# Graph attention, two layers: denominators of the last block summed by ones, its last output bank finished in two parts

## The chip, the cores and the metric

The kernel runs on one core of one Trainium2 chip, in one launch. The metric is the device time of an execution in microseconds (us); the median of several runs is compared. The engines are named as in the profile: PE is TensorE's matmul, PEld its loading of weights, DVE is VectorE, ACT is ScalarE, POOL is GpSimd, SP is SyncE (here only a queue for transfers).

## The reference

The input is a node matrix `x` of 4096 x 512 and an adjacency matrix of 4096 x 4096 of zeros and ones. Layer 0 is an encoder and decoder with sigmoid attention. Layer 1, in which the change lies, is graph attention with four heads of 128 features:

```python
    def _L1_gnn_ref(X, A, W, b, a_self, a_neigh):
        ...
        feats = jnp.einsum('nf,hfo->hno', X, W)
        e_s = jnp.einsum('hno,ho->hn', feats, a_self)
        e_n = jnp.einsum('hno,ho->hn', feats, a_neigh)
        logits = e_s[:, :, None] + e_n[:, None, :]
        logits = jnp.where(logits > 0, logits, LRELU_ALPHA * logits)
        logits = logits + NEG_INF * (1.0 - A)[None, :, :]
        attn = jax.nn.softmax(logits, axis=-1)
        out = jnp.einsum('hnm,hmo->hno', attn, feats)
        out = out + b[:, None, :]
        ...
        return jax.nn.relu(out)

    # --- layer 1 (adj_preln) ---
    h = jnp.maximum(_layernorm(x, axis=-1), 0.0)
    x = x + _L1_gnn_ref(h, adj, L1_gnn_W, L1_gnn_b, L1_gnn_a_self, L1_gnn_a_neigh)
```

For every head and target node the kernel needs two sums over all 4096 neighbours: the weighted sum of features, and the sum of the weights, by which it divides (the denominator).

## The kernel before, in words

All three attentions go through one function, `attention`. A block is one head and one half of the target nodes (TB = 2048 of them), so each attention has eight blocks. Inside a block the loop runs over 32 tiles `j` of 128 neighbours. One step makes a weight tile `e` of 128 neighbours x 2048 targets and uses it:

- SP loads the mask tile `a` (five buffers, so tile j's load waits for the release of tile j - 5).
- ACT computes a ReLU of the scores into `e` (L1045), and DVE adds a column and multiplies by the mask (L1046, the "mask product"). The pool has nine buffers for `e`.
- PE multiplies the feature block of tile `j` with `e` and accumulates into four banks `po` of 128 x 512 (L470). A matmul in float32 appears in the profile as two records.
- For the denominator each tile goes one of three ways, by the entry of the block in a table (`GAT_FIRST`, `GAT`, `GAT_LAST`): "moved" tiles are added into a buffer `w` by POOL's accumulating transfers (L490); tiles "by ones" are summed on PE against a column block of ones (L268, `add_to_den`, four matmuls of 32 columns into one bank `den`); all others are added on DVE into `acc` (L500; the profile calls its memory `R`). At the end of the block `w` and `acc` are summed by ones into `den` too.

Engines run their instructions in the order that a scheduler wrote down; a wait holds up everything behind it on the same engine.

The last block of the last attention ends differently from the others. Its last four tiles, 28 to 31, are not multiplied in the loop. They are kept in `late`, and their products come after the sums by ones, bank by bank (L533), so that PE has work while the denominators go their way: DVE copies `den` adding a small constant (L546) and inverts it (L547), SP stores the four rows to memory as `rinvs` (L549) and loads them back four times, spread over all partitions (L552). These spread rows are written over `acc`, which is free by then. Then `finish_gat` takes each bank in turn: DVE adds `ssum` and multiplies by the spread inverse (L1065), takes the maximum with the negative bias and adds the residual (L1066), and SP stores the result (L1067). The end of the program waits for these stores.

In this block `GAT_LAST` sends the odd tiles 3 to 23 to POOL and tiles 30 and 31 to the sums by ones; the other nineteen are added on DVE. A list `at_end` exists that holds additions back until all 32 mask products have been issued, but only for the encoder, by the condition `kept is not None`:

```python
                        if last and kept is not None and j >= NJ - 6:
                            at_end.append(e)
```

Of the kernel before, what the change touches and what calls it, by code (L numbers as in the profile page):

```python
# [34 lines left out]
ALU = mybir.AluOpType  # L35
# [4 lines left out]
N, F, H, D, P = 4096, 512, 4, 128, 128  # L40
IB = 512
NIB = N // IB
NJ = N // P
C = IB // P

TB = 2048
NTB = N // TB
SB = TB // IB
# [18 lines left out]
GAT_FIRST = (0, 2, 4, 6, 8, 10, 12, 14, 16, 18, 20, 22, 24), (30, 31)  # L67
GAT = tuple(range(3, 28, 2)), (31,), True

GAT_LAST = (3, 5, 7, 9, 11, 13, 15, 17, 19, 21, 23), (30, 31)  # L70

KEEP = 5

# [17 lines left out]
def kernel(ctx, tc, x, xT, adjT, w0, w0T, v0, wencT, wdecT, vecs, w1, w1T, a1, outT):  # L91
    nc = tc.nc
# [8 lines left out]
    R = [RS[:, i, :] for i in range(5)]  # L101
# [3 lines left out]
    def nodes(r, ib):  # L105
        return r[:, ib * IB:(ib + 1) * IB]

    def block(r, j):
        return r[:, j * D:(j + 1) * D]

    def bank():
        return psum.tile([P, IB], FP, name="ps")
# [111 lines left out]
    def attention(what, keep, pools, weights, values, row_of, out, finish, ebufs, modes=None, invert=None,  # L224
                  kept=None, sums=None, sums2=None, extras={}, row0=None, masks0=(), in_parts0=1,
                  finish_last=None, behind=(), fast=None):
# [38 lines left out]
        def add_to_den(den, t, start=False, stop=False):  # L265
            nonlocal last_ones
            for s in range(SB):
                last_ones = nc.tensor.matmul(den[s * 32:(s + 1) * 32, :], ones[:, 0:32], t[:, s * IB:(s + 1) * IB],  # L268
                                             start=start, stop=stop)
# [20 lines left out]
        def spread(h, tb, s):  # L290

            rb = spool.tile([P, IB], FP, name="rb", bufs=3 if fast is None else 2)
            hop.dma_start(rb, everywhere(rinvs[h][tb], 0, s * IB, IB))  # L293
            return rb

        def at(j, f, *args):

            later.setdefault(j, []).append(lambda: f(*args))
# [97 lines left out]
        for n, (h, tb) in enumerate(blocks):  # L396
            last = n == len(blocks) - 1
# [5 lines left out]
            if fast is None:  # L403
                po = [bank() for _ in range(SB - 1)]
            else:
                po, aux = (banks8[(n + k) % 2 * SB:((n + k) % 2 + 1) * SB] for k in range(2))
                if tb == 0:
                    fast[2](h)
            ahead, late = [], []
            adds, held, stores, at_end, next_row = [], [], [], [], None  # L410
            for j in range(NJ):
# [13 lines left out]
                else:  # L425
# [11 lines left out]
                    if stores and (store if n > 1 else j % KEEP == KEEP - 3):  # L437
                        k, t = stores.pop()
# [47 lines left out]
                if invert is not None:  # L486
                    if j in moved:

                        for into_half, e_half in in_parts(2, into, e):
                            nc.gpsimd.dma_start(into_half, e_half, **({"accum_op": ALU.add} if j > moved[0] else {}))  # L490
                    elif j in by_ones:
                        held.append(e)
                    else:
                        adds.append(e)
                        if last and kept is not None and j >= NJ - 6:
                            at_end.append(e)
                        elif len(adds) == 2:
                            nc.vector.tensor_add(acc, *adds)
                        elif len(adds) > 2:
                            nc.vector.tensor_add(acc, acc, e)  # L500

                    if j == NJ - 1:
                        for t in at_end:
                            nc.vector.tensor_add(acc, acc, t)

                    if held and j + 1 not in by_ones:
                        with tc.issue_after(last_main.ins):
                            for t in held:
                                add_to_den(den, t, not begun)
                                begun = True  # L510
                        held = []
                    if j == NJ - 1:
                        with tc.issue_after(last_ones.ins) if last_ones is not None else nullcontext():
                            if moved and not ends_later:
                                add_to_den(den, into, not begun)
                                begun = True
                            add_to_den(den, acc, not begun, not ends_later)
# [5 lines left out]
            if not last:  # L523

                at(EVICT if fast is None else 3, ending, h, tb, po, den if invert is not None else None,
                   4 if kept == "write" and n == 0 else 0)
                if ends_later:
                    at(1, add_to_den, den, into, False, True)
                rowb = next_row
                continue  # L530
            for s, b in enumerate(po):
                for k, t in late:
                    nc.tensor.matmul(b, block(values[h], k), t[:, s * IB:(s + 1) * IB], start=(k == 0),  # L533
                                     stop=(k == NJ - 1))
            if fast is not None:
                combined(h, tb, m)
            outs = [out(spool, h, tb, s, po[s]) for s in range(SB)] if finish_last is None else po
            if invert is None:
                for s, o in enumerate(outs):
                    rb = spread(h, tb, s)  # L540
# [11 lines left out]
                queue.dma_start(rb, everywhere(rinvs[h][tb], 0, s * IB, IB))  # L552
            for s, rb in enumerate(rbs):
                if finish_last is not None:
                    finish_last(h, tb, s, po[s], rb)
                    continue
                for f in finish:
                    f(spool, h, tb, s, outs[s], rb, True)

    def in_parts(n, *tiles):  # L560
        for i in range(n):
            yield tuple(t[:, i * TB // n:(i + 1) * TB // n] for t in tiles)
# [10 lines left out]
    with tc.tile_pool(name="keep", bufs=1) as keep:  # L573

        with tc.tile_pool(name="f_small", bufs=1) as small, tc.tile_pool(name="f_work", bufs=2) as work:
# [5 lines left out]
            for ib in range(NIB):  # L581
# [7 lines left out]
                for c in range(0, C, 1 if ib == 0 else C):  # L589
                    n = 1 if ib == 0 else C  # L590
# [11 lines left out]
            for ib in range(NIB):  # L602
# [34 lines left out]
                if ib == 0:  # L637

                    pw = bank1()
                    with tc.issue_after(last_pe.ins):  # L640
                        for h in range(H):
                            nc.tensor.matmul(pw[:, 2 * h:2 * h + 2], w0Ts[:, h, :], v0s[:, h, :],
                                             start=True, stop=True)
# [4 lines left out]
                for c in range(C):  # L648
                    j = ib * C + c
                    for k in range(2):  # L650
                        pv = heads_of(bank())
                        for h in range(2):
                            nc.tensor.matmul(pv[:, h, :], hT[:, 2 * k + h, c * P:(c + 1) * P], w0x[:, 2 * k + h, :],
                                             start=True, stop=True)
# [75 lines left out]
        with tc.tile_pool(name="enc", bufs=1) as spool:  # L730

            with tc.issue_after(last_copy.ins), tc.issue_after(masks0[-1][1].ins):
                attention("enc", keep, spool, tanh_weights, R[0:4], lambda h, tb: (rows[tb], h), out_enc,
                          (scaled, statistics), 6, lambda n: (ENC_FIRST, ENC_SECOND, ENC_THIRD, ENC)[min(n, 3)],
                          (TINY, ALU.max), "write", row0=row0, masks0=masks0,
                          extras={(2, 8): encoder_weights, (H * NTB - 1, 1): coefs_of_three,
                                  (H * NTB - 1, 4): bias_of_three, (H * NTB - 1, 6): scale_three,
                                  (H * NTB - 1, 9): product_ahead(0), (H * NTB - 1, 12): product_ahead(1)})
# [100 lines left out]
        with tc.tile_pool(name="dec", bufs=1) as spool:  # L839
            attention("dec", keep, spool, tanh_weights, xc, lambda h, tb: (rows[tb], h), out_dec, (scaled, elu), 5,  # L840
                      kept="read", behind=behind_it, fast=(z, xd, stationaries),
                      extras={(H * NTB - 1, 28): decoder_weights})
# [8 lines left out]
    with tc.tile_pool(name="l_small", bufs=1) as small, tc.tile_pool(name="l_work", bufs=2) as work:  # L851
# [41 lines left out]
        for fb in range(C):  # L893
            with tc.issue_after(last_pe.ins):
                for h in range(H):
                    k = 2 * (fb * H + h)
                    last_pe = nc.tensor.matmul(pw[:, k:k + 2], w1Ts[:, h, fb * P:(fb + 1) * P], a1s[:, h, :],
                                               start=True, stop=True)
# [62 lines left out]
        for ib in range(NIB):  # L961
            for c in range(C):
# [9 lines left out]
                j = ib * C + c  # L972
# [85 lines left out]
        nc.scalar.activation(o, o, AF.Relu, bias=vec_of("b")[:, h:h + 1])  # L1058
        nc.gpsimd.dma_start(nodes(outT[h * P:(h + 1) * P, :], tb * SB + s), o, accum_op=ALU.add)

    def finish_gat(h, tb, s, po, rb):

        x1b, nb = x1_last
        o = R[2][:, TB + s * IB:TB + (s + 1) * IB]
        nc.vector.scalar_tensor_tensor(o, po, ssum[:, h:h + 1], rb, ALU.add, ALU.mult)  # L1065
        nc.vector.scalar_tensor_tensor(o, o, nb, x1b[:, s * IB:(s + 1) * IB], ALU.max, ALU.add)  # L1066
        nc.sync.dma_start(nodes(outT[h * P:(h + 1) * P, :], tb * SB + s), o)  # L1067

    with tc.tile_pool(name="gat", bufs=1) as spool:
        x1_last = []  # L1070

        def load_last(load):
            x1_last.append(spool.tile([P, TB], FP, name="rowb", bufs=2))
            nc.sync.dma_start(x1_last[0], outT[(H - 1) * P:H * P, (NTB - 1) * TB:NTB * TB])
            x1_last.append(edge.tile([P, 1], FP, name="nb"))
            nc.vector.tensor_scalar_mul(x1_last[1], vec_of("b")[:, H - 1:H], -1.0)

        def add_bias(load):
            nc.scalar.activation(x1_last[0], x1_last[0], AF.Identity, bias=vec_of("b")[:, H - 1:H])

        with tc.issue_after(last_pe.ins):
            attention("gat", spool, spool, gat_weights, v1, lambda h, tb: (rowsg, tb * H + h), out_gat,
                      (scaled_gat, add_to_output), 7, lambda n: (GAT_FIRST, *[GAT] * (H * NTB - 2), GAT_LAST)[n],
                      (N * TINY, ALU.add), sums=R[2][:, 0:TB], sums2=(row0, R[2][:, TB:N]), row0=row0, in_parts0=3,
                      extras={(0, 1): rest_of_rows, (H * NTB - 1, NJ - 10): load_last, (H * NTB - 1, NJ - 4): add_bias},
                      finish_last=finish_gat)
# [42 lines left out]
```

## Time and profile before

| what | value |
|---|---|
| time, median of 3 runs | 3191.79 us (3190.47 to 3193.64) |
| the profiled execution's own time | 3192.33 us |
| its span | 3190.4 us, 30044 instructions |
| PE busy | 3139.7 us, 98% of the span, 10531 records |
| DVE busy | 2938.4 us, 92%, 2222 instructions |
| ACT busy | 2573.5 us, 81% |
| POOL busy | 522.3 us, 16% |
| mean PE clock over the span | 0.998 of full speed |

The profile is of one execution. Its times count from the start of its span, which is some 2 us shorter than the time of that execution; the end of the span is at 3190.4. A line such as L1046 is a line of the kernel before. Names are the program's (`e`, `den`, `acc`), and where a tile is a view of a larger memory, the larger one's name is shown: `R` holds `acc`, the spread inverses and the outputs of the last block. Busy shares are averages over a program with many stages. The last block runs from about 3065 us on (its first products on PE), and what matters for the change lies in its last 50 us, where the timeline of each engine and the chain of waits are read.

### The profile page before, as it was taken

How to read it: one execution, taken by the hardware profiler on the slowest of the kernel's cores; microseconds unless marked ns; L12 is line 12 of the kernel's file. 1: busy time of each engine (PE TensorE's matmuls, PEld its weight loads, DVE VectorE, ACT ScalarE, POOL GpSimd, SP SyncE). 2: the span in 40 equal slices, each digit the busy share in tenths (PEclk: the TensorE clock that was granted, in tenths of full speed). 3: DMA queues.
4: the chain of work that ended last, by engine and by line, in shares of the span. 5: the costliest groups of instructions: out<-in, count | busy, mean ns of one | idle time of the engine just before them, and what ended most of it. 6: DMA issues, size and time to landing. Idle time of an engine off the chain costs nothing.

```text
span 3190.4 us, 30044 instructions
## 1 busy us (share of the span) xinstructions
PE 3139.7 (98%) x10531; PEld 1368.4 (43%) x10531; DVE 2938.4 (92%) x2222; ACT 2573.5 (81%) x1825; POOL 522.3 (16%) x679
## 2 busy tenths in 40 slices
PE   7999999999999999999999999999999999999998
PEld 6334444444444463333333333458544444444443
DVE  7989999999998778999999999785699999999998
ACT  7999999999998449999999999466755665666663
POOL 3001211211211000010100100026312222222211
PEclk9999999999999999999999999999999999999999
DMA  9999978988987014444544454322579999899996
GB/s 211 199 194 254 267 209 232 268 223 231 264 226 200 20 47 146 160 164 148 166 162 161 139 169 145 104 98 74 151 191 229 216 222 242 220 211 232 233 210 163
DMA packets 215343, 590.28 MB, mean 185 GB/s; under 512 B 25912, under 2 KB 29016, under 8 KB 199192
## 3 DMA queue, kind: packets, MB, share of 16 engines
q0 software_dynamic: 70976, 231.94, 38.0%
q1 hardware_dynamic: 132200, 332.53, 30.3%
q10 hardware_dynamic: 12016, 23.90, 2.1%
q8 instruction: 82, 1.34, 0.2%
q14 instruction: 69, 0.57, 0.1%
HBM read 379.20 MB, written 84.30 MB: 145 GB/s over the span
## 4 chain that ended last, share of the span: by engine, by line
PE 54%; DVE 21%; issue 12%; ACT 8%; DMA 4%; DVEq 0%; POOL 0%; ACTq 0%; POOLq 0%; SPq 0%
PE ps L332 22%; PE ps L470 14%; PE ps L718 7%; DVE e L1046 6%; DVE R L500 6%; ACT e L566 5%; DVE e L568 4%; PE den L332 3%; PE ps L951 3%; DVE acc L500 3%; ACT e L567 3%; DMA a<-mask 3%; PE den L268 1%; PE ps L800 1%; DMA acc<-e 1%
## 5 line engine op out<-in xcount | busy, mean ns | idle before, releaser
L470 PE MATMUL ps<-e,R 128*128 128x512 f32 x3992 | 1736.8, 595 | 21.3 <-DVE e L568 17.2
L470 PEld LDWEIGHTS ps<-e,R 128*128 128x128 f32 x3992 | 754.0, 190 | 1000.1 <-issue 923.4
L568 DVE TENSOR_TENSOR e<-e,a 128x2048 f32<-128x2048 f32 (+1 forms) x470 | 1049.5, 2260 | 78.6 <-ACT e L567 65.1
L566 ACT ACTIVATE e<-rowb,score 128x2048 f32<-128x2048 f32 (+1 forms) x470 | 909.2, 1969 | 20.6 <-PE ps L332 9.0
L567 ACT ACTIVATE e<-e 128x2048 f32<-128x2048 f32 (+1 forms) x470 | 866.6, 1879 | 6.5 <-DVE e L568 3.2
L332 PE MATMUL ps<-e,R 128*64 128x512 f32 x2624 | 746.8, 592 | 1.6 <-DVE e L568 1.5
L1045 ACT ACTIVATE e<-rowb,nq,jcol 128x2048 f32<-128x2048 f32 x224 | 459.8, 2088 | 263.5 <-DMA w<-e 130.8
L1046 DVE SCALAR_TENSOR_TENSOR e<-e,jcol,a 128x2048 f32<-128x2048 f32 (+1 forms) x265 | 591.8, 2264 | 2.8 <-ACT e L1045 2.8
L332 PEld LDWEIGHTS ps<-e,R 128*64 128x64 f32 x2624 | 241.9, 137 | 319.8 <-issue 316.2
L500 DVE TENSOR_TENSOR R<-R,e 128x2048 f32<-128x2048 f32 x128 | 291.6, 2278 | 0.0
L500 DVE TENSOR_TENSOR acc<-acc,e 128x2048 f32<-128x2048 f32 x122 | 278.6, 2283 | 1.0
L490 POOL DMA_DIRECT2D w<-e x178 | 149.1, 847 | 611.9 <-DMA w<-e 335.1
L718 PE MATMUL ps<-R,w 128*128 128x512 f32 x512 | 220.8, 592 | 0.6 <-DVE w L692 0.6
L490 POOL DMA_DIRECT2D acc<-e x142 | 119.1, 893 | 518.5 <-DMA acc<-e 232.2
L718 PEld LDWEIGHTS ps<-R,w 128*128 128x128 f32 x512 | 97.1, 190 | 123.0 <-issue 116.7
L332 PE MATMUL den<-e,R 128*64 128x512 f32 x320 | 149.8, 592 | 0.0
L332 PE MATMUL ps<-e,w 128*64 128x512 f32 x288 | 138.1, 592 | 0.7 <-DVE e L568 0.7
L293 POOL DMA_DIRECT2D rb<-rinvs x60 | 34.5, 579 | 518.8 <-DVE R L682 453.6
L951 PE MATMUL ps<-w1x,hT 128*128 128x260 f32 x512 | 115.5, 384 | 1.4 <-ACT hT L929 1.4
L332 PE MATMUL ps<-t,w 128*64 128x512 f32 x336 | 111.2, 592 | 1.1 <-DVE t L341 1.1
L951 PEld LDWEIGHTS ps<-w1x,hT 128*128 128x128 f32 x512 | 96.5, 190 | 19.9 <-issue 3.4
L332 PE MATMUL ps<-t,R 128*64 128x512 f32 x192 | 90.2, 592 | 0.0
(205 smaller groups left out, 2103.9 us busy)
## 6 DMA issues: line engine op xcount, KB each, us to landing
a<-mask SPq DMA_DIRECT2D x720, 256.0 KB, 4.3
w<-e POOLq DMA_DIRECT2D x178, 512.0 KB, 6.7
acc<-e POOLq DMA_DIRECT2D x142, 512.0 KB, 7.0
e<-ekeep SPq DMA_DIRECT2D x48, 1024.0 KB, 5.0
ekeep<-e SPq DMA_DIRECT2D x36, 1024.0 KB, 8.3
mask<-in_adjT POOLq DMA_DIRECT2D x8, 2048.0 KB, 106.0
rowb<-rows SPq DMA_DIRECT2D x16, 1024.0 KB, 7.5
rb<-rinvs POOLq DMA_DIRECT2D x60, 256.0 KB, 4.6
```

The costliest lines, as they stand in the source:

```text
L293: hop.dma_start(rb, everywhere(rinvs[h][tb], 0, s * IB, IB))
L332: last_half = nc.tensor.matmul(b[g * HD:(g + 1) * HD, :], weight, x, start=start, stop=stop)
L470: last_main = nc.tensor.matmul(b, block(values[h], j), e[:, s * IB:(s + 1) * IB], start=(j == 0), stop=(j == NJ - 1))
L490: nc.gpsimd.dma_start(into_half, e_half, **({"accum_op": ALU.add} if j > moved[0] else {}))
L500: nc.vector.tensor_add(acc, acc, e)
L566: nc.scalar.activation(e, rowb, AF.Tanh, bias=column(score[:, 1], j, h), scale=0.5)
L567: last_act = nc.scalar.activation(e, e, AF.Exp, scale=0.5)
L568: last_dve = nc.vector.tensor_mul(e, e, a)
L718: last = nc.tensor.matmul(z, w[:, fb, o * P:(o + 1) * P], nodes(src[fb], ib), start=(fb == 0), stop=(fb == C - 1))
L951: m = nc.tensor.matmul(banks[k][:, 0:2 * DX], hT[:, fb, c * P:(c + 1) * P], w1x[:, fb, 2 * k:2 * k + 2, :].rearrange("p h x -> p (h x)"), ...
L1045: last_act = nc.scalar.activation(e, rowb, AF.Relu, bias=column(nq, j, h), scale=column(jcol, j, h))
L1046: last_dve = nc.vector.scalar_tensor_tensor(e, e, column(jcol2, j, h), a, ALU.add, ALU.mult)
```

## The change

Three things are altered, all in the last block of the last attention.

Tiles 28 and 29 are summed by ones on PE as tiles 30 and 31 are, and no longer added on DVE. The additions of tiles 26 and 27 stay on DVE, but come after the mask products of all tiles, since the condition on `at_end` no longer asks for the encoder. (For the encoder nothing changes; the decoder has no denominators.) And the last of the four banks is handled in two halves of 256 columns: its late products, its two finishing instructions, and its store.

```diff
-GAT_LAST = (3, 5, 7, 9, 11, 13, 15, 17, 19, 21, 23), (30, 31)
+GAT_LAST = (3, 5, 7, 9, 11, 13, 15, 17, 19, 21, 23), (28, 29, 30, 31)
...
-                        if last and kept is not None and j >= NJ - 6:
+                        if last and j >= NJ - 6:
                             at_end.append(e)
...
+            def last_parts(s):
+                n = 2 if s == SB - 1 and finish_last is not None else 1
+                return [slice(i * IB // n, (i + 1) * IB // n) for i in range(n)]
+
             for s, b in enumerate(po):
-                for k, t in late:
-                    nc.tensor.matmul(b, block(values[h], k), t[:, s * IB:(s + 1) * IB], start=(k == 0),
-                                     stop=(k == NJ - 1))
+                for part in last_parts(s):
+                    for k, t in late:
+                        nc.tensor.matmul(b[:, part], block(values[h], k), t[:, s * IB:(s + 1) * IB][:, part],
+                                         start=(k == 0), stop=(k == NJ - 1 and part.stop == IB))
...
                 if finish_last is not None:
-                    finish_last(h, tb, s, po[s], rb)
+                    for part in last_parts(s):
+                        finish_last(h, tb, s, part, po[s][:, part], rb[:, part])
                     continue
...
-    def finish_gat(h, tb, s, po, rb):
+    def finish_gat(h, tb, s, part, po, rb):
 
         x1b, nb = x1_last
-        o = R[2][:, TB + s * IB:TB + (s + 1) * IB]
+        o = R[2][:, TB + s * IB:TB + (s + 1) * IB][:, part]
         nc.vector.scalar_tensor_tensor(o, po, ssum[:, h:h + 1], rb, ALU.add, ALU.mult)
-        nc.vector.scalar_tensor_tensor(o, o, nb, x1b[:, s * IB:(s + 1) * IB], ALU.max, ALU.add)
-        nc.sync.dma_start(nodes(outT[h * P:(h + 1) * P, :], tb * SB + s), o)
+        nc.vector.scalar_tensor_tensor(o, o, nb, x1b[:, s * IB:(s + 1) * IB][:, part], ALU.max, ALU.add)
+        nc.sync.dma_start(nodes(outT[h * P:(h + 1) * P, :], tb * SB + s)[:, part], o)
```

In the changed kernel the lines behind the edit shift: L533 becomes L538, L546 and L547 become L551 and L552, L1046 becomes L1052, L1065 to L1067 become L1071 to L1073, and the held-back additions are at L504.

## The prediction

> **What bounds the kernel now.** The page comes first: PE is busy 98% of the span, DVE 92%. Those are averages over 3190.4 us, and the change touches only the last 50 us or so, so the rest is read there. First the chain of waits, limited to the last 30 us. Its columns are start, length, what.
>
> ```profile
> 3160.05 2.28 DVE R L500
> 3162.33 0.07 DVE e L1046
> 3162.40 2.11 issue
> 3164.52 2.28 DVE R L500
> 3166.80 2.27 DVE e L1046
> 3169.07 0.04 issue
> 3169.12 2.78 PE den L268 x24
> 3171.90 6.22 PE ps L533 x14
> 3178.12 0.16 SPq L552
> ...
> 3178.34 3.88 DMA R<-rinvs
> ```
>
> The end is set first by DVE (weight tiles L1046 and additions L500 in turn), then by three sums by ones on PE, then by the denominators. The chain puts 3171.90 to 3178.12 down to products L533, but the DVE and SP rows name what really runs there: the copy of `den` (L546) at 3172.05, the reciprocal (L547) from 3172.77 for 3.35, the store of `rinvs` issued at 3176.15, its landing some 1.8 us later. After the broadcast lands, L1065 and L1066 run one after another to 3187.30. Second, the timeline of PE:
>
> ```profile
> 3159.59 2.74 PE L470 MATMUL ps<-e,R 128*128 128x512 f32 x6
> 3164.65 1.67 PE L268 MATMUL den<-e,ones 128*32 128x512 f32 x8 [2.32 <-DVE e L1046]
> 3166.26 2.08 PE L533 MATMUL ps<-e,R 128*128 128x512 f32 x2
> 3169.12 1.06 PE L268 MATMUL den<-e,ones 128*32 128x512 f32 x8 [0.79 <-DVE e L1046]
> 3170.00 1.04 PE L268 MATMUL den<-w,ones 128*32 128x512 f32 x8
> 3170.86 1.04 PE L268 MATMUL den<-R,ones 128*32 128x512 f32 x8
> ```
>
> PE runs without a gap up to 3162.33 (one block of 169 records from 3089.64), then waits twice for DVE: tile 30's sum starts at 3164.65, tile 31's at 3169.12. Third, the timeline of DVE just there:
>
> ```profile
> 3153.32 2.34 DVE L1046 SCALAR_TENSOR_TENSOR e<-e,jcol,a 128x2048 f32<-128x2048 f32 x1
> 3155.59 2.28 DVE L500 TENSOR_TENSOR R<-R,e 128x2048 f32<-128x2048 f32 x1
> 3157.79 2.35 DVE L1046 SCALAR_TENSOR_TENSOR e<-e,jcol,a 128x2048 f32<-128x2048 f32 x1
> 3160.05 2.28 DVE L500 TENSOR_TENSOR R<-R,e 128x2048 f32<-128x2048 f32 x1
> ```
>
> Counted back from the last L1046, these are tile 28, the addition of 27, tile 29, the addition of 28. Each addition costs 2.20 (start to next start). So up to 3162 PE is the bound, and from there to the denominators DVE is late by its additions. Last, the table by stages (length, PE, PEld, DVE, ACT, POOL busy, clock, DMA):
>
> ```profile
> 3162.30:3169.10 6.80, 3.71 (x11) 0.66 (x10) 6.76 (x4) 0.00 (x0) 0.00 (x0) 0.75 0.00 0
> ```
>
> PE's clock falls to 0.75 on average in this hole.
>
> **What the skill says.** "TensorE: Matmul & The Clock Gate", Part 1, says an idle PE is clocked at half until some microseconds of activity release it. The trace agrees: the two L533 records of 3166.26 took 2.08, the first two at 3171.83 took 1.13. "TensorEngine Tiling (Array Packing)", Available Configurations, allows four tiles of 128x32 side by side; the trace agrees, since four sums by ones (8 records) take 0.86, what one full product (2 records of 0.428) takes. "VectorE: DVE Perf Modes", on the trn2 errata, says each instruction has a fixed cost beside its elements. The trace agrees: a 128x512 copy from PSUM takes 677 ns, a 128x256 one 421, not half.
>
> **The change part by part.** The built order of the changed program differs only at the end of the last block, on PE, DVE and SP; ACT and POOL issue the same instructions.
>
> *DVE.* Tile 27 ends at 3151.21 as before. Tiles 28 to 31 follow at 2.27 each (the spacing of the pair at 3137.67): four additions, 26 to 29, no longer stand between, 4 x 2.20 = 8.8, so tile 31 ends at 3160.3 instead of 3169.07. Two of the four additions are gone, those of 26 and 27 follow and end at 3164.7. ACT covers this, since its last tile ends at 3150.24; so do the masks: the last is issued at 3146.8 and all DMA is quiet from about 3154 (share 0.09 in 3154 to 3156), 4 us before DVE wants it.
>
> *PE.* Added: two more sums by ones. All four tiles are ready or come in time when the products of tile 27 let PE go at 3162.17, so the waits go and the clock stays up. Four tiles, `w` and `acc` make six sums. From other blocks: the first 0.88 (3062.89 to 3063.77), 0.86 each for the next, 0.97 for the last up to the next product (3170.86 to 3171.83): 0.88 + 4 x 0.86 + 0.97 = 5.29. The late products start at 3167.46 instead of 3171.83. The sum of `acc` comes up at 3166.5; its wait for DVE (3164.7) has 1.8 us to spare, and `w`'s transfers landed by 3154.
>
> *Denominators.* The last sum ends at 3167.53 (start plus 1.04), L546 starts 0.15 later as before, at 3167.68: **4.37 us earlier**. The reciprocal, the store and the broadcast move whole. First L1065: 3177.1; the last bank's turn on DVE, 3185.77 before, comes at 3181.4.
>
> *Late products.* Before, one of 16 ran in the hole; now all 16 follow. The twelve wide ones take 12 x 0.857 = 10.28. The eight 128x256 have no row of their own; L951 (128x260) takes 115.5/512 = 0.226 a record, so some 0.222 x 16 = 3.55, against 3.43 for the four wide ones. Lower bound 3.43, upper bound a whole record each (0.382), 6.1. PE ends at 3167.46 + 10.28 + 3.55 + 0.17 (drain: 0.384 less 0.222) = 3181.46, against 3184.97. **PE moves by only 3.5 us**, and becomes what is late next: bank 3 can be read at 3181.6, when DVE is free at 3181.4.
>
> *Two parts.* In the built program the first half's L1065 counterpart waits for the same PE count as the whole bank (the last product of the second half), and the second half's has no wait at all. So nothing overlaps with PE. What remains is four instructions of 256 columns for two of 512. By the copies' slope (1.0 ns per column) one takes 748 - 256 = 492 ns, 0.41 when the next doesn't depend on it: 3 x 0.41 + 0.49 = 1.73, against 1.53 (3185.77 to 3187.30). Bounds: 1.4 with no fixed cost, 2.8 with all of it. A fifth transfer out is issued on SP: the first half's goes 0.41 ahead (0.34 to issue), so the second isn't held. Landing 2.0 at 256 KB; the 8 KB store of `rinvs` needed 1.8, so half the size gains 0 to 0.2; I take 0.
>
> *Sum.* DVE ends at 3181.62 + 1.73 = 3183.35 instead of 3187.30, 3.95 earlier. The tail of 3.1 to the span's end stays. Span 3190.4 - 3.95 = 3186.45; the profiled execution's own time, 3192.33, becomes 3188.4. It stands 0.54 above the median 3191.79, so **3187.9**.
>
> **The rivals.**
> *The narrow products are dear.* Each costs a whole record because its weight load (0.19) no longer hides under it: +2.6, time 3190.5. L951, with the same load before each 260-column product, speaks against it.
> *DVE is late anyway (ends slower).* If something but the additions paces tiles 28 to 31, say a late mask or buffer, tile 31 still ends at 3169.07, and now two additions stand behind it: `acc` at 3173.5, its sum 1.04, L546 at 3174.8 against 3172.05. Time 3191.79 + 2.75 = 3194.5. It costs from a DVE delay of 1.8 us on and is a loss from 1.8 + 4.37 = 6.2. ACT's early end and the quiet DMA speak against it.
> *The two parts do overlap.* If the first half could be read while PE fills the second, DVE would still be free only at 3181.4 and end at 3183.15: 3187.7. Hardly to be told apart by time.
> *A large gain.* PE is packed from 3089.64 on and keeps 5.29 + 13.8 of work after 3162.17, so no saving on DVE can bring more than about 4.2; beyond that only differences between runs.
>
> **How the numbers follow.** The forecast 0.72, the dear narrow products 0.07, DVE late 0.04, the overlap 0.05, and 0.12 for a median shifted by 6 us or more by differences between runs, which three runs within 3.2 us make unlikely but can't exclude. Bounds on the forecast: -0.5 (narrow work at its lower bounds, quicker landing), +2.6 (products) and +1.1 (finish). Range 3185.2 to 3191.0, leaving out the late DVE. A measurement of this kernel can tell about 0.2%, 6.4 us, from no change; a gain of 3.9 is 0.12%. Every case worked out above lies within it: 0.88. Only shifted medians leave it: 0.08 to faster (under 3185.4, which the forecast is nearer to), 0.04 to slower.
>
> **What would show it.** In the changed profile: tile 31 ends near 3160.3 and additions near 3164.7; PE has no gap from 3089.6 to about 3181.5, six sums by ones in 5.3 from 3162.2, all at full clock; L546 near 3167.7; narrow product records start every 0.22; the first half's read starts after PE's last product, at 3181.6; four DVE instructions of 0.49. Wrong would be: a PE wait before the sum of `acc`, narrow records 0.38 apart, a first half read before PE has ended, or a part of the timeline before 3151 that differs.

## The result, and the profile after

| | before | changed |
|---|---|---|
| time, median of 22 runs each | 3191.52 us (3189.65 to 3194.06) | 3187.52 us (3185.68 to 3190.32) |
| ratio, with its 95% interval | | 0.9988 (0.9983 to 0.9994) |
| span of the profiled execution | 3190.4 us | 3187.4 us |
| its own time | 3192.33 us | 3189.23 us |

The change gains 4.0 us, 0.12% (1.9 to 5.4 us by the interval); 3187.9 was forecast. The two profiled executions differ by only 3.0 us in span, since in the second the last loop itself came to its end 1.35 us later. Below, therefore, a second measure stands beside the medians: **the tail**, from the end of the loop's last product on PE (L470) to the end of the span. It is 3190.4 - 3162.33 = 28.07 us before and 3187.4 - 3163.68 = 23.72 us after, 4.35 less. Spans are read to 0.1 us here, so a tail is good to 0.05 and a difference of two tails to 0.1; with the two spans to the nanosecond, 3190.367 and 3187.444, this difference is 4.27.

The timeline of PE in the changed kernel (start, length, what, number of records):

```profile
3136.47 27.20 PE L470 MATMUL ps<-e,R 128*128 128x512 f32 x63
3163.60 3.64 PE L268 MATMUL den<-e,ones 128*32 128x512 f32 x32
3167.06 1.04 PE L268 MATMUL den<-w,ones 128*32 128x512 f32 x8
3167.92 1.04 PE L268 MATMUL den<-R,ones 128*32 128x512 f32 x8
3168.89 14.02 PE L538 MATMUL ps<-e,R 128*128 128x512 f32 x40
```

No line carries an idle time in brackets any more: loop, six sums (3163.60 to 3168.89, 5.29) and late products follow each other. The timeline of DVE in the same kernel:

```profile
3150.22 11.38 DVE L1052 SCALAR_TENSOR_TENSOR e<-e,jcol,a 128x2048 f32<-128x2048 f32 x5
3161.53 4.60 DVE L504 TENSOR_TENSOR R<-R,e 128x2048 f32<-128x2048 f32 x2
3169.11 0.69 DVE L551 TENSOR_SCALAR dsb<-den 128x512 f32<-128x512 f32 x1 [2.98 <-PE den L268]
...
3182.95 0.88 DVE L1071 SCALAR_TENSOR_TENSOR R<-ps,ssum,R 128x256 f32<-128x256 f32 x2 [0.20 <-PE ps L538]
3183.74 0.87 DVE L1072 SCALAR_TENSOR_TENSOR R<-R,nb,rowb 128x256 f32<-128x256 f32 x2
```

Five mask products now run without a break (tiles 27 to 31), the two additions behind them, and DVE is done with both at 3166.13, before the sum of `acc` begins at 3167.92. The last bank waits 0.20 for PE. The chain of waits has turned over accordingly. The sums on PE are still in it, but what follows them on the way of the denominators (the row of `R<-rinvs` above all) is not:

```profile
3149.94 13.73 PE ps L470 x32
3163.67 5.29 PE den L268 x48
3168.96 13.97 PE ps L538 x40
3182.93 0.03 issue
3182.95 0.88 DVE R L1071 x2
```

And in the table by stages the stretch that had a clock of 0.75 and a PE busy for 3.71 of 6.80 us now reads:

```profile
3162.30:3169.10 6.80, 6.80 (x53) 1.97 (x52) 3.79 (x2) 0.00 (x0) 0.00 (x0) 1.00 0.01 2
```

### The profile page after: what moved, and what is told of

Read it like the earlier page. It is cut to its first block, busy times and chain, and to the rows that moved or that the text cites. A ratio compares the mean times of both kernels' runs of the same rounds, so it can differ in the third digit from the quotient of the medians.

```text
span 3187.4 us, 30095 instructions
## 1 busy us (share of the span) xinstructions
PE 3140.5 (99%) x10555; PEld 1371.4 (43%) x10555; DVE 2934.3 (92%) x2222; ACT 2572.8 (81%) x1825; POOL 522.3 (16%) x679
## 4 chain that ended last, share of the span: by engine, by line
PE 73%; DVE 10%; ACT 7%; issue 7%; DMA 2%; DVEq 0%; ACTq 0%; POOL 0%; POOLq 0%
PE ps L470 32%; PE ps L332 22%; PE ps L724 7%; ACT e L572 4%; DVE e L574 4%; PE den L332 3%; PE ps L957 3%; DVE acc L500 3%; ACT e L573 2%; PE den L268 2%; DMA a<-mask 1%; DVE R L500 1%; DVE e L1052 1%; PE ps L806 1%; PE ps L467 1%
## 5 line engine op out<-in xcount | busy, mean ns | idle before, releaser
L470 PE MATMUL ps<-e,R 128*128 128x512 f32 x3992 | 1736.0, 595 | 22.5 <-DVE e L574 18.5
L470 PEld LDWEIGHTS ps<-e,R 128*128 128x128 f32 x3992 | 754.3, 190 | 1000.4 <-issue 924.0
L1052 DVE SCALAR_TENSOR_TENSOR e<-e,jcol,a 128x2048 f32<-128x2048 f32 (+1 forms) x265 | 591.2, 2262 | 2.8 <-ACT e L1051 2.8
L500 DVE TENSOR_TENSOR R<-R,e 128x2048 f32<-128x2048 f32 x124 | 282.2, 2276 | 0.0
```

The lines of the kernel that those rows point to most:

```text
L470: last_main = nc.tensor.matmul(b, block(values[h], j), e[:, s * IB:(s + 1) * IB], start=(j == 0), stop=(j == NJ - 1))
L1052: last_dve = nc.vector.scalar_tensor_tensor(e, e, column(jcol2, j, h), a, ALU.add, ALU.mult)
```

## The experiments

All tails in one table. "Loop's end" is the end of the last L470 product in the profiled execution; it varies by 6 us between these executions. No edit makes that difference: in all twelve traces the loop's last 208 records on PE take the same 89.43 us without a gap, so it arises before them, ahead of every edit. It is about as large as the spread of one kernel's runs, and the reason for using the tail. Each tail is that of one execution. Where PE works without a wait, its pieces repeat to some 0.02 us from kernel to kernel; the time from the store of `rinvs` to the first read of its broadcast varies from 5.0 to 5.3.

| kernel | loop's end | span | tail | median | ratio to before (95%) |
|---|---|---|---|---|---|
| before | 3162.33 | 3190.4 | 28.07 | 3191.52 | |
| changed | 3163.68 | 3187.4 | 23.72 | 3187.52 | 0.9988 (0.9983 to 0.9994) |
| parts_only | 3162.04 | 3189.6 | 27.56 | 3192.28 | 0.9999 (0.9991 to 1.0007) |
| one_part | 3163.92 | 3187.8 | 23.88 | 3188.61 | 0.9986 (0.9979 to 0.9992) |
| ones_in_place | 3164.49 | 3188.3 | 23.81 | 3189.17 | 0.9990 (0.9983 to 0.9997) |
| behind_only | 3166.56 | 3196.2 | 29.64 | 3192.57 | 1.0003 (0.9995 to 1.0011) |
| dve_extra1 | 3161.04 | 3185.4 | 24.36 | 3188.32 | 0.9987 (0.9981 to 0.9994) |
| dve_extra3 | 3161.87 | 3193.9 | 32.03 | 3195.32 | 1.0010 (1.0003 to 1.0017) |
| six_ones | 3162.32 | 3187.8 | 25.48 | 3189.28 | 0.9991 (0.9983 to 0.9999) |
| moved25 | 3163.36 | 3186.3 | 22.94 | 3186.62 | 0.9984 (0.9977 to 0.9990) |
| extra3_busy | 3160.53 | 3189.8 | 29.27 | 3193.38 | 1.0004 (0.9996 to 1.0012) |
| moved27 | 3160.93 | 3184.2 | 23.27 | 3187.66 | 0.9985 (0.9979 to 0.9992) |

The medians were taken in four groups, each with its own runs of before (3191.52, 3192.05, 3191.78, 3192.39), so they are compared by ratio.

### One part of the change at a time

**parts_only**: the changed kernel with both other edits undone.

```diff
-GAT_LAST = (3, 5, 7, 9, 11, 13, 15, 17, 19, 21, 23), (28, 29, 30, 31)
+GAT_LAST = (3, 5, 7, 9, 11, 13, 15, 17, 19, 21, 23), (30, 31)
-                        if last and j >= NJ - 6:
+                        if last and kept is not None and j >= NJ - 6:
```

> Only the two-part finish of the last bank; additions and sums by ones as in the kernel before. Measure: the tail, from the end of the loop's last product on PE (L470) to the end of the span: before 28.07 us, changed kernel 23.73. Theory (the gain comes from DVE's four additions leaving the path; the parts bring nothing but a slightly shorter last transfer): the last bank's turn on DVE is still set by the denominators, four narrow instructions take 1.66 instead of 1.53, the end behind them is 0.3 shorter: tail 27.9, time within 0.5 us of before. Rival (the parts overlap with PE and carry the gain): tail down by 1 us or more, the first narrow read before PE's last product ends.

The tail was 27.56. DVE's last instruction ends 2.83 before the span's end here and 3.06 before it in the kernel before: the last transfer, half as large, is over 0.23 sooner. The four narrow instructions take 0.13 longer than the two wide ones. The rest of the 0.5 is not the parts' doing: a broadcast that landed 0.13 earlier, and a first pair of L1071 that is 0.23 shorter. The time did not move.

**one_part**: the changed kernel, last bank in one piece.

```diff
-                n = 2 if s == SB - 1 and finish_last is not None else 1
+                n = 1
```

> The changed kernel without the two parts: last bank finished in one piece of 512 columns. Theory: PE ends 0.1 earlier (16 wide products 13.7 instead of 13.85), DVE's turn is free at the same time as PE is done, finish 1.53 instead of 1.66, last transfer 0.3 longer: tail 23.7 to 23.9 against 23.73, time within 0.5 us of the changed kernel. Rival (parts matter): tail longer by 0.8 or more.

The tail was 23.88, 0.16 longer, or 0.09 with the spans to the nanosecond (3187.773 against 3187.444). So the parts are worth some 0.1 us in the tail, in both comparisons, and nothing that the times can tell.

**ones_in_place**: four tiles by ones, but the additions of 26 and 27 back in their old places.

```diff
-                        if last and j >= NJ - 6:
+                        if last and kept is not None and j >= NJ - 6:
```

> The changed kernel with the additions of tiles 26 and 27 back between the mask products; tiles 28 to 31 still by ones. Theory: only two of the four additions are gone from before tile 31, so tile 31 ends 4.5 us later than in the changed kernel, some 2.5 us after the loop's last product; PE reaches its sum by ones 2.6 us after that product, so it hardly waits: tail 23.7 to 24.0; the move behind the mask products is worth nothing once four tiles go by ones. Rival (mask products late cost PE one for one): tail up by 2 to 4 us, to 26 to 28, with PE waiting for DVE before the sum of tile 31.

The tail was 23.81, within 0.1 of the changed kernel. The last lines of DVE's mask products and PE's sums in this kernel:

```profile
3159.94 6.86 DVE L1052 SCALAR_TENSOR_TENSOR e<-e,jcol,a 128x2048 f32<-128x2048 f32 x3
3164.42 3.64 PE L268 MATMUL den<-e,ones 128*32 128x512 f32 x32
```

DVE finishes tile 31 at 3166.80, 2.3 after the loop's end, and PE sums the four tiles in 3.64 without a wait, since tile 31 is the last of the four and comes up at about 3167.0. The four sums by themselves cover DVE's lateness. Moving the additions is worth nothing beside them, though only some 0.2 us are to spare.

**behind_only**: the additions behind the mask products (four of them, 26 to 29), tiles 30 and 31 by ones as before.

```diff
-GAT_LAST = (3, 5, 7, 9, 11, 13, 15, 17, 19, 21, 23), (28, 29, 30, 31)
+GAT_LAST = (3, 5, 7, 9, 11, 13, 15, 17, 19, 21, 23), (30, 31)
```

> Only the additions (26 to 29, four of them) put behind the mask products, with the two parts; tiles 30 and 31 by ones as before. Theory: DVE still has all its work, the last addition ends about 6.8 us after the loop's last product (four at 2.2 after tile 31), PE does the sums of 30, 31 and w in 2.6 and then waits some 4 us for the sum of acc: denominators about 1.7 us earlier than before, late products start at 7.8 after the loop's end and end about 22 after it or later if the clock falls in the hole: tail 26 to 27.5, a gain of 0.6 to 2. Rival (moving the additions is what gains): tail within 0.5 of 23.73.

This missed: the tail was 29.64, longer than before by 1.57, where 0.6 to 2 less was expected. PE's timeline and two of its clock stretches:

```profile
3168.23 1.04 PE L268 MATMUL den<-w,ones 128*32 128x512 f32 x8
3173.70 1.94 PE L268 MATMUL den<-R,ones 128*32 128x512 f32 x8 [4.43 <-DVE R L504]
3175.57 16.06 PE L538 MATMUL ps<-e,R 128*128 128x512 f32 x40
```

```profile
3169.30:3173.70 4.40, 0.00 (x0) 0.00 (x1) 4.31 (x2) 0.00 (x0) 0.00 (x0) 0.91 0.00 0
3175.60:3178.00 2.40, 2.40 (x7) 1.14 (x4) 2.19 (x2) 0.00 (x0) 0.00 (x0) 0.50 0.00 0
```

The wait of 4.43 is as large as expected ("some 4 us"). What was not priced is the work after it at half clock: the sum of `acc` takes 1.94 instead of 1.04, the late products 16.06 instead of 14.02, 2.9 us together. Without the sums by ones, the move of the additions is a loss in the tail; the time shows no difference.

### The spare time, and the price beyond it

**dve_extra1** and **dve_extra3**: the changed kernel with one or three more instructions on DVE behind the additions. The maximum of `acc` with itself leaves it as it is. The edit of the first (the second has `range(3)`):

```diff
                         for t in at_end:
                             nc.vector.tensor_add(acc, acc, t)
+                        if last and kept is None:
+                            for _ in range(1):
+                                nc.vector.tensor_max(acc, acc, acc)
```

> The changed kernel with one more DVE instruction of the additions' length (maximum of acc with itself, 2.2 us) behind the two held-back additions. Theory: the sum of acc has 1.8 us to spare, so of 2.2 us only 0.4 to 0.5 reaches the end: tail 24.1 to 24.3 against 23.73. Rival A (DVE sets the end one for one): tail 25.9. Rival B (PE alone sets it): tail 23.7.

> The changed kernel with three such extra DVE instructions (6.6 us to 6.8 us). Theory, the slow rival's price: 1.8 us are spare, the rest, 4.8 to 5, goes to the end, and up to 1.7 more if PE's clock falls in the hole of about 5 us before the sum of acc: tail 28.5 to 30.2, slower than the kernel before (28.07) by 0.4 to 2.1 us. Rival (PE alone sets the end): tail 23.7.

With one, PE waits 0.41 before the sum of `acc` and the tail is 24.36: of 2.3 us more on DVE 0.64 reaches the end, a little more than the 0.4 to 0.5 expected. So some 1.7 were spare, where the prediction had 1.8. With three it is 32.03, above the range that was expected (30.2). PE again, with three:

```profile
3171.36 1.94 PE L268 MATMUL den<-R,ones 128*32 128x512 f32 x8 [5.06 <-DVE R L507]
```

The late products take 16.15 there. Against the changed kernel the sum of `acc` starts 5.25 later (9.49 after the loop's end instead of 4.24), but the tail grows by 8.3.

**extra3_busy**: the kernel with three more instructions, and six products nobody needs put into the hole on PE, in front of the sum of `acc`. What is added to dve_extra3:

```diff
-                            add_to_den(den, acc, not begun, not ends_later)
+                            if last and kept is None:
+                                filler = bank()
+                                for _ in range(6):
+                                    with tc.issue_after(last_ones.ins):
+                                        last_ones = nc.tensor.matmul(filler, block(values[h], 0), e[:, 0:IB],
+                                                                     start=True, stop=True)
+                            with tc.issue_after(last_ones.ins) if last_ones is not None else nullcontext():
+                                add_to_den(den, acc, not begun, not ends_later)
```

> The kernel with three extra DVE instructions, and six filler products (12 records, 5.1 us, into a free bank that nothing reads) put on PE in the hole before the sum of acc. DVE's delay stays as it is (with three extra instructions: tail 32.03, the sum of acc starts 9.49 after the loop's last product and takes 1.9, the late products 16.15). Theory (about 3 us of that kernel's loss are PE's clock at half after the hole): the sum of acc takes 1.0 again, the late products 14.0, tail 29.0 (23.72 plus 5.25 of later start). Rival (the loss is the wait for DVE alone, products slow for another reason): tail 32 or longer.

```profile
3164.89 5.42 PE L524 MATMUL ps<-e,R 128*128 128x512 f32 x12
3170.23 1.06 PE L268 MATMUL den<-R,ones 128*32 128x512 f32 x8
3171.23 14.02 PE L548 MATMUL ps<-e,R 128*128 128x512 f32 x40
```

The tail falls from 32.03 to 29.27 by adding work. The sum is back at 1.06 and the late products at 14.02 with DVE's delay unchanged. Of the 8.3 us that three instructions cost, then, 2.8 is the clock and 5.5 the wait. (The sum starts 0.2 later here than in dve_extra3, behind the added products; by the lengths alone, 0.9 on the sum and 2.1 on the products, the clock's part is 3.0.)

### What bounds the changed kernel

**six_ones**: tiles 26 and 27 by ones too; DVE has no held-back additions.

```diff
-GAT_LAST = (3, 5, 7, 9, 11, 13, 15, 17, 19, 21, 23), (28, 29, 30, 31)
+GAT_LAST = (3, 5, 7, 9, 11, 13, 15, 17, 19, 21, 23), (26, 27, 28, 29, 30, 31)
```

> The changed kernel with tiles 26 and 27 summed by ones too, so no held-back additions. Theory (PE is packed from the loop to its last product and is the bound, or level with the denominators): two more sums of 0.87 on PE, 1.7 us later at the end: if both stand before the end of the loop the loop ends 1.7 later and the tail keeps 23.7; time 1.7 us over the changed kernel. DVE's 4.4 us less bring nothing. Rival (DVE still is the bound): faster than the changed kernel.

All six sums stand behind the loop in the trace (48 records from 3162.25), and the tail is 25.48, 1.76 longer, two sums' worth. DVE waits 9.23 for PE before it copies `den`. PE is the bound, and what DVE is relieved of brings nothing more.

**moved25**: tile 25 goes from DVE to POOL's transfers, tile 28 from the sums by ones back to DVE, behind the mask products.

```diff
-GAT_LAST = (3, 5, 7, 9, 11, 13, 15, 17, 19, 21, 23), (28, 29, 30, 31)
+GAT_LAST = (3, 5, 7, 9, 11, 13, 15, 17, 19, 21, 23, 25), (29, 30, 31)
```

> The changed kernel with tile 25 added by POOL's transfers instead of DVE, and tile 28 added on DVE (held back) instead of by ones: DVE does as much as in the changed kernel, PE one sum less. Theory (PE's work between the loop and the last product sets the end, with the denominators level): sums, late products and denominators all 0.86 us earlier: tail 22.9. Condition: the additions end about 2.5 after the loop's last product, PE reaches the sum of acc at 3.5; the last transfer into w lands by 3160 to 3162 and the sum of w comes at 2.6 after the loop. Rival (the denominators' chain or the transfers into w set the end): tail 23.7 or more, with PE waiting for a transfer before the sum of w.

```profile
3163.29 2.78 PE L268 MATMUL den<-e,ones 128*32 128x512 f32 x24
3165.89 1.04 PE L268 MATMUL den<-w,ones 128*32 128x512 f32 x8
3166.75 1.04 PE L268 MATMUL den<-R,ones 128*32 128x512 f32 x8
```

One sum less on PE, none of the others waits, and the tail is 22.94, 0.78 less than in the changed kernel. It has the best ratio of all, 0.9984, but its interval overlaps that of the changed kernel: that it beats the kernel before is shown by the times, that it beats the changed one only by the tail.

**moved27**: one step further, tile 27 by POOL too, tiles 30 and 31 by ones, three additions held back.

```diff
-GAT_LAST = (3, 5, 7, 9, 11, 13, 15, 17, 19, 21, 23), (28, 29, 30, 31)
+GAT_LAST = (3, 5, 7, 9, 11, 13, 15, 17, 19, 21, 23, 25, 27), (30, 31)
```

> The kernel with tile 25 added by POOL, taken one step further: tile 27 by POOL's transfers too, tiles 30 and 31 by ones, tiles 26, 28 and 29 added on DVE behind the mask products. Theory (PE's packed work sets the end): one more sum less, tail 22.1 against 22.94. Rival (the transfers into w become the bound): tile 27's two half transfers wait for tile 25's, which start at 3151.7 and 3154.9 there and take 6 each, so they land at about 3164 and 3167 while the sum of w comes at 3165; PE waits 1 to 2 us before it, tail 22.9 to 24, no gain.

The rival holds. The tail is 23.27, 0.33 more than in moved25. The late products start 4.69 after the loop's end, against 4.36 in moved25; with one sum of 0.86 less it would have been 3.50, so PE lost 1.2 in its sums, more than was saved. The waits name the transfers into `w` (PEld is held before its loads of weights, PE before its products; the two overlap):

```profile
PEld den L268 <- DMA w<-e: 1.1, 1, 1.1
PE den L268 <- DMA w<-e: 0.2, 1, 0.2
```

## Why the prediction was right

By its own steps, with times counted from the loop's end (3162.33 in the prediction, 3163.68 in the changed kernel):

- *DVE no longer late.* Tile 31 was to end 2.0 before it, the additions 2.4 after it; they end 2.1 before and 2.45 after. No mask and no ACT tile came in between.
- *Six sums in 5.29.* They take 5.29. (The "four sums" of 8 records and 0.86 that the prediction speaks of are the four matmuls of one such sum.)
- *Denominators 4.37 earlier.* L551 starts 5.43 after the loop's end instead of 9.72: 4.29. The missing 0.08 is a gap between the last full product and the first sum that was not counted.
- *PE's end 3.5 earlier, and PE the next to be late.* Its end goes from 22.64 to 19.23: 3.41. The narrow records start every (14.02 - 24 x 0.428 - 0.38)/15 = 0.224, priced 0.222. The rival of dear narrow products (0.38 each) is out.
- *No overlap of the two parts.* The first half is read at 3182.95, PE's last product ends at 3182.91. Whether an overlap would help was not tried.
- *Finish 1.73.* It took 1.66 (3182.95 to 3184.61).
- *The tail behind it stays 3.1.* It became 2.83, in each of the ten kernels with two parts, against 3.06 in the two without. This term was mis-sized: the gain of a half-sized last transfer was bounded at 0 to 0.2 and taken as 0; it is 0.23.

Predicted tail 24.12, measured 23.72; of the 0.40 between them 0.27 is that last term (3.1 to 2.83), 0.07 the finish, and the rest is rounding of the span.

The steps are the test here, more than the median. The interval of the gain, 1.9 to 5.4 us, would have fitted many other sums, and the median of the kernel before itself moved from 3191.79 with 3 runs to 3191.52 with 22; that the forecast came within 0.4 us is in part luck. The prediction put what a measurement can tell from no change at 0.2%; with 22 runs of each, a gain of 0.12% stands clear of no change.

The prediction credited the edits together. The experiments divide them: the two more sums by ones carry nearly all of it (parts_only, 27.56, and ones_in_place, 23.81, differ in them alone). The move of the additions brings 0.1 at most beside them and is a loss alone, and the parts bring some 0.1. The remaining 0.4 lies between before and parts_only (0.13 and 0.23, above): later broadcasts in the one execution of before, and none of the edits. The times agree as far as they reach: ones_in_place is faster than the kernel before, parts_only and behind_only are not.

The slow rival (DVE late before the sum of `acc`) did not occur, but its mechanism is real, and it was sized too low. The prediction let DVE's delay cost one for one from 1.8 us on. For the 6.9 us of dve_extra3 that would be a tail of 28.9; it was 32.0. The missing term is PE's clock after the hole, 2.8 of these 3.1 us by extra3_busy, although the prediction had read that same clock in the profile of before. There it cost the end nothing: one sum and one product took some 1.7 longer under it (1.61 instead of 0.87, 2.08 instead of 1.13), and PE still waited 0.79 for DVE behind them. The expectation for behind_only failed by the same term.

## What to carry to other kernels

When one engine waits for another near the end, ask which work can go to the waiting engine: the sums by ones filled a hole in PE, kept its clock up and shortened DVE's list at once, while reordering DVE's list alone only moved the hole. A hole on PE is to be priced with the half clock after it, here 1.7 us of PE's time after a hole of 2.32 and some 3 after holes of 4.43 and 5.06, beside the hole itself. And where runs of a long kernel scatter by more than an edit is worth, measure the edit from a fixed event in the trace just before it.

## What was not expected of the hardware

The half clock outlasts a short hole. After a hole of 2.32 us (before, 3162.33 to 3164.65) the eight records of a sum took 1.6 us from start to next start instead of 0.87; after holes of 4.43 and 5.06 the sum and the next 4 us of products ran at 0.50. Stretches of the table, from before and two from behind_only:

```profile
3164.97:3168.39 3.42, 3.36 (x10) 0.50 (x2) 3.42 (x2) 0.00 (x0) 0.00 (x0) 0.50 0.00 0
3172.87:3173.70 0.83, 0.00 (x0) 0.00 (x1) 0.78 (x1) 0.00 (x0) 0.00 (x0) 0.50 0.00 0
3173.70:3179.69 5.99, 5.99 (x13) 2.05 (x14) 3.88 (x2) 0.00 (x0) 0.00 (x0) 0.50 0.00 0
```

In before it lasts 3.41 us. In behind_only (3172.87 to 3179.70) and dve_extra3 (3170.72 to 3177.55) it lasts twice as long, and begins 0.83 and 0.64 us before PE works again. Half of the busy time in it is what it costs: 3.36 / 2 = 1.7, 5.99 / 2 = 3.0 and, in dve_extra3, 6.18 / 2 = 3.1, which agrees with the 1.7, 2.9 and 3.0 by which sums and products were longer.

Holes of 0.41 (dve_extra1) and 0.79 (before, 3168.33 to 3169.12) left full rate behind them. Where above 0.79 it begins was not tried, and the length of a hole alone does not decide it. Near 188 us each of the twelve kernels has a hole of 2.04 to 2.15 us on PE: in the changed kernel the clock behind it is 1.00 (189.20 to 192.70), in moved25 it is 0.50 (191.72 to 195.10). Where the hole falls goes with it. Within one execution the half clock starts at whole multiples of 3.413 us from each other (before: 308.02, 929.24, 3164.97), as if it were set anew for each stretch of that length. In moved25, dve_extra3 and ones_in_place the hole near 188 us lies within one such stretch, and the half clock follows; in the nine others it lies across two, and none follows. So a hole of some 2 us can cost in one execution and not in the next. That is a reading of twelve traces, not an experiment, and it is not the whole rule: in before, the half clock from 929.24 to 932.65 follows 3.4 us in which PE was never idle, most of them spent on products of a single column (L697).
